# Masked attention on one core: the symmetric scores made once, their maxima sent through DRAM

## The chip, the cores and the metric

The kernel runs on one core of a Trainium2 chip. The metric is the device time of one execution, in microseconds. The core has four engines that compute: TensorE (PE in the profile; PEld is its loading of weights), VectorE (DVE), ScalarE (ACT) and GpSimd (POOL). SyncE (SP) issues the transfers between DRAM and the core's memory. Each engine works through its own list of instructions in order, and waits where an operand or a buffer isn't ready. TensorE writes its results into PSUM, eight banks of 512 float32 per partition.

## The reference

Four layers follow each other, all in float32. B is 8 samples, a sample is 256 x 512, and each layer's result goes on to the next with a residual. The change is in the first one, with 8 heads of 32 channels over 512 positions:

```python
q = xt @ Wq.T
scores = scale * jnp.einsum('bhqd,bhkd->bhqk', qh, qh)
cmask = mask[:, None, None, :]
rmask = mask[:, None, :, None]
logits = (scores * cmask + (1.0 - cmask) * NEG) * rmask
attn = jax.nn.softmax(logits, axis=-1)
ctx = jnp.einsum('bhqk,bhkd->bhqd', attn, qh)
out = ctx @ Wo.T
```

Queries and keys are the same vectors, so the scores of a head are a symmetric matrix. The mask takes keys away (cmask), and a masked query (rmask) weighs all keys alike: its context is the mean over the positions. The second layer is a modulated attention without a mask (16 heads, 256 positions), the third a scan of 256 time steps of an oscillator network, and the fourth a recurrent cell (GRU) over the same steps. The last two run as one loop, the scans.

## The kernel before

The program has two parts. The first, `attention`, does the first two layers for the eight samples; the second, `scans`, does the two scans. The second part starts when the first is done.

`attention` is one loop over steps g, from -5 to 78, with the instructions of each step written out in a fixed order (`manual_schedule`), so every engine's list follows the order of the calls. A sample takes U = 8 steps of masked attention: two halves e of four heads each, four steps per half. `at(g, rel, 8)` gives the sample b and the place in its eight steps for work that is rel steps late. The modulated attention of a sample runs about ten steps behind, so that in a step the two layers of neighbouring samples alternate on all engines.

The masked attention of sample b, by steps:

- `load` (g = 8b - 7): x and the mask row, the latter broadcast to all partitions (`mk`).
- `project` (8b - 5, 8b - 4): q for one half (`psq`), masked (`qm`, on VectorE) and copied (`qt`, on ScalarE); `project_out` turns it into `qtok` a step later.
- `maxima0` (from 8b - 4 on): scores of 128 positions against all 512, one PSUM bank per head (tile `n`, L204), and a maximum over each bank by VectorE (L209) into `mxp0`. After four steps `rows0` turns the maxima into rows (`pm`, `mrow`).
- `weights0` (from 8b on): the scores once more, transposed, with columns for 256 queries at a time (tile `s`, L226). A second product with two rows (L231) adds the mask and takes the maximum away inside PSUM. Its operands are `neg` and `mrow`. ScalarE's Exp (L238) writes `ex`.
- `values0` (8b + 1 to 8b + 9): the products of `ex` with the values and with ones (`pc`, L153), in two halves, and `weigh0` with a reciprocal and a product on VectorE.
- `masked_out` (8b + 9): the output projection (`pso`) and the residual.

The modulated attention follows: `normalize`, `modulate`, six `qkv` parts (`psqkv`), each of q and k normalized by `qkv_norm` (a reduction `s16` on VectorE, then three GpSimd instructions, one of them a pow, ending with `qr`) and turned by `qkv_out` in the next step (`ptqk`); then for each of four groups of heads `maxima1`, `rows1`, `weights1`, `values1`; and `modulated_out` (`psx`) with `modulated_turn` (`ptx`), which writes into `x2T`. That tile, 32 KB in each partition, holds the attention's whole result for the scans.

Seven PSUM banks go round for all of this (`bank`), and one is held for `pc` of the masked attention. At step 65 the tiles of the masked attention are given up and `follow` loads the scans' weights into their place.

Of the kernel before, what the change touches and what calls it, by code (L numbers as in the profile page):

```python
# [14 lines left out]
P = 128  # L15
# [9 lines left out]
def attention(ctx, tc, cst, x, cond, wqT, woT, w_emb, b_emb, g_norm, w_qkv, g_q, g_k, w_out, x2T, follow):  # L25
# [27 lines left out]
    ps_s = ctx.enter_context(tc.tile_pool(name="a_ps_s", bufs=7, space=PSUM))  # L53
    ps_c = ctx.enter_context(tc.tile_pool(name="a_ps_c", bufs=1, space=PSUM))

    def bank(shape, name):
        return ps_s.tile(shape, F32, tag="s", name=name)
# [3 lines left out]

    xs, mks = {}, {}

    def load(b):
        xs[b] = two.tile([P, 2, D], F32, tag="x", name=f"x_{b}", bufs=4)
        nc.sync.dma_start(xs[b], x[b].rearrange("(k p) t -> p k t", p=P))
        mks[b] = fone.tile([P, D], F32, tag="mk", name=f"mk_{b}")
        nc.sync.dma_start(mks[b], cond[b].partition_broadcast(P))
# [35 lines left out]

    rowm = wp.tile([P, 3], F32, name="rowm")
    nc.vector.memset(rowm, 0.0)
    nc.vector.memset(rowm[:, 1:2], 1.0)
    nc.vector.memset(rowm[:, 2:3], -1.0)
    for h in range(4):
        nc.vector.memset(rowm[32 * h : 32 * h + 1, 0:1], NEG)  # L110
        nc.vector.memset(rowm[32 * h : 32 * h + 1, 1:2], -NEG)
        nc.vector.memset(rowm[32 * h : 32 * h + 1, 2:3], 1.0)
# [48 lines left out]
    def weigh(pc, out, n):  # L161
        r = sm.tile([P, 256], F32, tag="r", name=f"r_{n}", bufs=2)
        nc.vector.reciprocal(r, pc[:, 1, :])
        nc.vector.tensor_mul(out, pc[:, 0, :], r)


    qms, qtoks, negs, mrows, exs0, ctxTs = {}, {}, {}, {}, {}, {}

    def project(b, e):
        if e == 0:  # L170
            qms[b] = ftwo.tile([P, 2, D], F32, tag="qm", name=f"qm_{b}")
            qtoks[b] = ftwo.tile([P, NJ, 256], F32, tag="qtok", name=f"qtok_{b}")
            negs[b] = ftwo.tile([P, D], F32, tag="neg", name=f"neg_{b}")
        ps = bank([P, D], f"psq_{b}_{e}")
        for k in range(2):
            nc.tensor.matmul(
                ps, lhsT=wq_sb[:, k, e * P : (e + 1) * P], rhs=xs[b][:, k, :], start=(k == 0), stop=(k == 1)
            )
        nc.vector.tensor_mul(qms[b][:, e, :], ps, mks[b])
        qt = line(f"qt_{b}_{e}")  # L180
        nc.scalar.copy(qt, ps)
        if e == 0:
            nc.gpsimd.tensor_scalar(negs[b], mks[b], rowm[:, 0:1], rowm[:, 1:2], ALU.mult, ALU.add)
        return qt
# [6 lines left out]

    def maxima0(b, e, qc):

        if qc == 0:
            nc.gpsimd.tensor_copy(
                mxp0[e].rearrange("p q (h i) -> p q h i", i=32)[:, :, :, 0],
                condT[:, :, b].unsqueeze(2).to_broadcast([P, NJ, 4]),
            )
        qm = qms[b]
        ss = []  # L200
        for h in range(4):
            r = 32 * h
            s = bank([P, D], f"n0_{b}_{e}_{qc}_{h}")
            nc.tensor.matmul(  # L204
                s, lhsT=qm[r : r + 32, e, qc * P : (qc + 1) * P], rhs=qm[r : r + 32, e, :], start=True, stop=True
            )
            ss.append(s)
        for h in range(4):
            nc.vector.tensor_reduce(mxp0[e][:, qc, 32 * h + 1 : 32 * h + 2], ss[h], AX.X, ALU.max)  # L209

    def rows0(b, e):
        pt = bank([P, NJ, P], f"pm0_{b}_{e}")
        for qc in range(NJ):
            nc.tensor.transpose(pt[:, qc, :], mxp0[e][:, qc, :], ident)
        mrows[b, e] = ftwo.tile([P, D], F32, tag="mrow", name=f"mrow0_{b}_{e}")
        nc.scalar.activation(mrows[b, e], pt.rearrange("p q n -> p (q n)"), AF.Copy, scale=rowm[:, 2:3])

    def weights0(b, e, qh, kp):
        qm, neg, mrow = qms[b], negs[b], mrows[b, e]
        qs = slice(256 * qh, 256 * qh + 256)  # L220
        ss = [bank([P, 2, 256], f"s0_{b}_{e}_{qh}_{kp}_{h}") for h in range(4)]
        for i in range(2):
            kc = slice((2 * kp + i) * P, (2 * kp + i + 1) * P)
            for h in range(4):
                r = 32 * h
                nc.tensor.matmul(  # L226
                    ss[h][:, i, :], lhsT=qm[r : r + 32, e, kc], rhs=qm[r : r + 32, e, qs], start=True, stop=False
                )
            for h in range(4):
                r = 32 * h  # L230
                nc.tensor.matmul(  # L231
                    ss[h][:, i, :], lhsT=neg[r : r + 2, kc], rhs=mrow[r : r + 2, qs], start=False, stop=True
                )
        exs = exs0.setdefault((b, e, qh), [])
        exs.append([])
        for h in range(4):
            ex = ftwo.tile([P, 2, 256], F32, tag="ex", name=f"ex0_{b}_{e}_{qh}_{kp}_{h}", bufs=12)
            nc.scalar.activation(ex, ss[h], AF.Exp, scale=SC)  # L238
            exs[-1].append(ex)

    pc0s = {}

    def values0(b, e, qh, half):
        if half == 0:
            if (e, qh) == (0, 0):
                ctxTs[b] = fone.tile([P, 2, D], F32, tag="ctxT", name=f"ctxT_{b}")
            pc0s[b, e, qh] = ps_c.tile([P, 2, 256], F32, tag="c", name=f"pc0_{b}_{e}_{qh}")
        pc = pc0s[b, e, qh]
        o = e * P
        values(pc, half, lambda k, h: qtoks[b][:, k, o + h * DH : o + (h + 1) * DH], exs0[b, e, qh])  # L250

    def weigh0(b, e, qh):
        pc = pc0s[b, e, qh]
        weigh(pc, ctxTs[b][:, e, qh * 256 : (qh + 1) * 256], f"0_{b}_{e}_{qh}")
# [159 lines left out]
    def modulated_turn(b, m, x2):  # L414
        pt = bank([P, NJ, P], f"ptx2_{b}_{m}")
        for j in range(NJ):
            nc.tensor.transpose(pt[:, j, :], x2[:, j * P : (j + 1) * P], ident)
        nc.scalar.copy(x2T[:, :, b, m * P : (m + 1) * P], pt)
# [6 lines left out]
    for b in range(B):  # L425
        per = 2 if b >= B - 2 else 1
        norms.append(U * b + U + (1 if b == B - 1 else 2))
        start = norms[b] + (2 if b != B - 2 else 3)
        for i, part in enumerate(PARTS):
            parts.setdefault(start + i // per, []).append((b, *part))  # L430
        HEADS.append(start + len(PARTS) // per)
        OUT.append(HEADS[b] + 6)
# [19 lines left out]
    with tc.manual_schedule():  # L452
        for g in range(-5, OUT[-1] + 3):
# [8 lines left out]
            if a := at(g, 0, U):  # L462
                weights0(a[0], a[1] // 4, a[1] // 2 % 2, a[1] % 2)
# [5 lines left out]
            if a := at(g, U + 1):  # L469
                masked_out(a[0])  # L470
# [9 lines left out]
            if a := heads(g, 1):  # L480
                rows1(*a)
            a, a1 = at(g, -4, U), heads(g, 0)
            soon = a and a[1] % 4 == 3
            if a and soon:
                maxima0(a[0], a[1] // 4, a[1] % 4)
            if a1 and not soon:
                maxima1(*a1)
            for part, lines in made:
                if lines:
                    qkv_norm(*part, *lines)  # L490
                    left["qkv", *part] = lines[1]
            if a2 := heads(g, 2):
                values1(*a2)
            if a2 := heads(g, 1):
                weights1(*a2)

            if (a2 := at(g, 1, U)) and a2[1] % 2 == 0:
                values0(a2[0], a2[1] // 4, a2[1] // 2 % 2, 0)
            behind = None
            if (a2 := at(g, 2, U)) and a2[1] % 2 == 0:  # L500
                behind = a2[0], a2[1] // 4, a2[1] // 2 % 2
                values0(*behind, 1)
            if a and not soon:
                maxima0(a[0], a[1] // 4, a[1] % 4)
            if a1 and soon:
                maxima1(*a1)
            if behind:
                weigh0(*behind)
            if soon:
                rows0(a[0], a[1] // 4)  # L510
            if (a2 := at(g, -7)) and a2[0] > 1:
                load(a2[0])
            if g == U * B + 1:
                first.close()
                follow()

# [390 lines left out]
def tile_kernel(  # L907
# [9 lines left out]
    x2T = cp.tile([P, NJ, B, T], F32, name="x2T")  # L917
# [34 lines left out]
    with ExitStack() as a:  # L952
        def follow():
            pool = ctx.enter_context(tc.tile_pool(name="s_weights", bufs=1, side="right", reuse_waits="tile"))
            cst["weights"] = scan_weights(pool, nc, cT, w_ih, w_hh)

        attention(a, tc, cst, x, cond, wqT, woT, w_emb, b_emb, g_norm, w_qkv, g_q, g_k, w_out, x2T, follow)
    with ExitStack() as s:
        scans(s, tc, cst, bias, b_ih, b_hh, x2T, out)
# [42 lines left out]
```

## Time and profile before

| | us |
|---|---|
| median of three runs | 3042.43 |
| lowest, highest | 3040.55, 3043.27 |
| profiled execution, its own time | 3040.15 |
| its span in the profile | 3038.4 |
| first instruction of the scans' loop (ic, L698) | 961.38 |
| last masked_out (first residual add, L264) | 853.92 |

Times inside the profile count from the start of the span. PE is busy 94% of the span, DVE 66%, ACT 53%, POOL 32%. The granted TensorE clock is 0.986 of full speed on the mean. The page divides the span into 40 slices of 76 us and gives each a digit, the busy share in tenths. A line of a group reads: line, engine, operation, what it writes and reads, count, then busy time in all and the mean ns of one, then the idle time of the engine just before it and what ended that. TensorE's float32 products stand as two records each in the trace.

### The profile page before, as it was taken

The page shows a single profiled execution, that of the slowest core. Times are in us where ns is not written, and L with a number is a line of the kernel's source. Part 1 is how long each engine was busy: PE and PEld are TensorE (multiplying, and loading weights), DVE is VectorE, ACT ScalarE, POOL GpSimd, SP SyncE. Part 2 cuts the span into 40 slices and gives each one's busy share as a digit, 9 for nine tenths or more (in the row PEclk, how much of TensorE's full clock was granted, in tenths as well). Part 3 has the DMA queues.
Part 4 walks back from the last instruction along what each step waited for, and adds up shares of the span by engine and source line. Part 5 has one row for each costly group of instructions (what it writes and reads, how often), then busy time and mean ns, then how long its engine had stood idle before and what let it go on. Part 6 is the DMA issues. An engine that isn't in the chain of part 4 may idle for free.

```text
span 3038.4 us, 165918 instructions
## 1 busy us (share of the span) xinstructions
PE 2847.2 (94%) x70330; PEld 2070.0 (68%) x70330; DVE 2002.5 (66%) x9090; ACT 1599.9 (53%) x8347; POOL 986.8 (32%) x2905
## 2 busy tenths in 40 slices
PE   8999999999988899999999999999999999999997
PEld 5455555555545677777777777777777777777775
DVE  4444444544434677777777777777777777777774
ACT  2333433433433566666666666666666666666652
POOL 0021111111221344444444444444444444444442
PEclk8999999999999999999999999999999999999999
DMA  3000000000040000000000000000000000000000
GB/s 129 5 1 1 12 11 1 12 11 1 2 98 2 4 7 6 7 6 6 7 6 7 6 6 7 6 7 6 6 7 6 7 6 6 7 6 7 6 6 7
DMA packets 17759, 35.31 MB, mean 12 GB/s; under 512 B 2144, under 2 KB 10860, under 8 KB 17012
## 3 DMA queue, kind: packets, MB, share of 16 engines
q1 hardware_dynamic: 17012, 24.69, 3.0%
q8 instruction: 550, 9.01, 1.2%
q14 instruction: 197, 1.61, 0.2%
HBM read 20.49 MB, written 4.19 MB: 8 GB/s over the span
## 4 chain that ended last, share of the span: by engine, by line
PE 62%; DVE 26%; ACT 6%; issue 4%; POOL 2%; ACTq 0%; DMA 0%; SPq 0%; POOLq 0%; DVEq 0%
PE pg L733 19%; PE ic L698 17%; PE psqkv L301 5%; DVE icT L890 5%; PE pc L153 5%; DVE qn L891 5%; ACT tT L598 4%; DVE hqs L851 3%; PE s L226 3%; DVE own L748 3%; DVE sqmm L847 2%; PE n L204 2%; DVE v L750 2%; PE psx L401 2%; DVE mxp L209 2%
## 5 line engine op out<-in xcount | busy, mean ns | idle before, releaser
L698 PE MATMUL ic<-cT_sb,tT 128*8 128x128 f32 x32736 | 1088.6, 273 | 82.2 <-ACT tT L598 44.6
L698 PEld LDWEIGHTS ic<-cT_sb,tT 128*8 128x8 f32 x32736 | 758.6, 89 | 344.0 <-ACT tT L598 272.0
L733 PE MATMUL pg<-whh_sb,hz 128*32 128x128 f32 x24576 | 818.5, 274 | 50.7 <-DVE hz L778 17.5
L598 ACT ACTIVATE tT<-qn 128x16 f32<-128x16 f32 x2046 | 440.2, 216 | 646.0 <-DVE qn L891 567.5
L733 PEld LDWEIGHTS pg<-whh_sb,hz 128*32 128x32 f32 x24576 | 667.4, 110 | 125.0 <-DVE hz L778 124.8
L890 DVE STREAM_TRANSPOSE icT<-ic 128x64 f32<-128x64 f32 x2048 | 503.7, 246 | 70.5 <-PE ic L698 64.9
L891 DVE SCALAR_TENSOR_TENSOR qn<-icT,hqs 128x16 f32<-128x16 f32 x2048 | 350.4, 171 | 70.1
L693 POOL TENSOR_TENSOR W<-W,cx 128x128 f32<-128x128 f32 x765 | 297.2, 389 | 256.7 <-ACT cx L679 256.7
L686 POOL TENSOR_TENSOR W<-cx,us 128x128 f32<-128x128 f32 x255 | 117.1, 459 | 446.1 <-ACT cx L679 446.1
L847 DVE SCALAR_TENSOR_TENSOR sqmm<-sqmm,qn 128x32 f32<-128x32 f32 x768 | 153.5, 200 | 152.2 <-ACT sqmm L836 123.1
L209 DVE TENSOR_REDUCE mxp<-n 128x1 f32<-128x512 f32 x256 | 158.7, 683 | 132.0 <-PE n L204 132.0
L851 DVE TENSOR_TENSOR hqs<-W,sqmm 128x32 f32<-128x32 f32 x1020 | 200.1, 196 | 46.1 <-DVE own L773 1.0
L238 ACT ACTIVATE ex<-s 128x512 f32<-128x512 f32 x256 | 132.1, 603 | 157.0 <-PE s L231 157.0
L712 PE MATMUL gi<-wih_sb,x3T 128*32 128x384 f32 (+2 forms) x3072 | 202.4, 379 | 0.5 <-POOL x3T L903 0.5
L324 POOL TENSOR_SCALAR r<-s 128x16 f32<-128x16 f32 x32 | 6.5, 204 | 604.0 <-DVE s L322 603.7
L679 ACT ACTIVATE cx<-qn 128x32 f32<-128x32 f32 x1280 | 200.9, 213 | 0.1
L301 PE MATMUL psqkv<-wqkv_sb,xnT 128*128 128x512 f32 x384 | 181.8, 620 | 0.0
L679 ACT ACTIVATE cx<-p 128x32 f32<-128x32 f32 x1020 | 149.8, 217 | 32.2 <-DVE p L846 1.4
L356 DVE TENSOR_REDUCE mxp<-n 128x2 f32<-128x512 f32 x128 | 79.6, 685 | 107.7 <-PE n L348 107.7
L226 PE MATMUL s<-qm 32*128 32x256 f32 x1024 | 139.4, 406 | 6.8 <-DVE mxp L209 6.8
L679 ACT ACTIVATE cx<-q 128x32 f32<-128x32 f32 x1020 | 145.5, 213 | 0.0
L748 DVE STREAM_TRANSPOSE own<-pg 128x128 f32<-128x128 f32 x256 | 84.9, 332 | 91.3 <-PE pg L733 91.3
(149 smaller groups left out, 3593.5 us busy)
## 6 DMA issues: line engine op xcount, KB each, us to landing
x<-in_x SPq DMA_DIRECT2D x8, 512.0 KB
out<-o SPq DMA_DIRECT2D x256, 16.0 KB
wqkv_sb<-in_L_cond_W_qkv SPq DMA_DIRECT2D x1, 3072.0 KB
wih_sb<-in_L_cond_W_ih SPq DMA_DIRECT2D x4, 768.0 KB
whh_sb<-in_L_cond_W_hh SPq DMA_DIRECT2D x4, 768.0 KB
mk<-in_cond SPq DMA_DIRECT2D x8, 256.0 KB
wemb<-in_L_cond_W_emb SPq DMA_DIRECT2D x4, 512.0 KB
wout_sb<-in_L_cond_W_out SPq DMA_DIRECT2D x1, 1024.0 KB
```

Of the source, the lines that this page charges most:

```text
L209: nc.vector.tensor_reduce(mxp0[e][:, qc, 32 * h + 1 : 32 * h + 2], ss[h], AX.X, ALU.max)
L226: nc.tensor.matmul(ss[h][:, i, :], lhsT=qm[r : r + 32, e, kc], rhs=qm[r : r + 32, e, qs], start=True, stop=False)
L301: nc.tensor.matmul(ps, lhsT=xnTs[b][:, c, m * P : (m + 1) * P], rhs=wqkv_sb[:, c, part * D : (part + 1) * D], start=(c == 0), stop=(c == N ...
L598: nc.scalar.activation(tT, src[:, half * HM : (half + 1) * HM, :], AF.Tanh)
L679: nc.scalar.activation(c[:, i], x, AF.Copy, scale=f)
L693: nc.gpsimd.tensor_tensor(W[:, i + 1 : 5], W[:, i + 1 : 5], c, ALU.add)
L698: nc.tensor.matmul(ps[32 * j : 32 * j + B, :], lhsT=tT[k // HM][:, k % HM, :], rhs=cT_sb[:, k, j * P : (j + 1) * P], start=(k == 0), stop= ...
L733: nc.tensor.matmul(pg_ps[rows(j), :], lhsT=hzs[tau % 3][:, k, 32 * g : 32 * g + 32], rhs=whh_sb[:, k, g, j * P : (j + 1) * P], start=((k, ...
L847: stt(mm, sq, LIN[s], qs, ALU.subtract, ALU.mult)
L851: nc.vector.tensor_sub(hq, W[:, s], mm)
L890: nc.vector.transpose(icT.rearrange("p m n -> p (m n)"), ic[:, half * 64 : half * 64 + 64])
L891: stt(qn[:, m2, :], icT[:, :, 0:B], IC[s], hq[:, m2, :], ALU.mult, ALU.add)
```

## The change

- `scores0` makes the scores of 128 positions against all 512 once (L198 of the changed kernel), and ScalarE copies the four heads' banks into a tile `sc` of 4 x 512 per partition (L203). Six such tiles are kept, so the scores stay from the step in which they are made until their products with the values.
- `maxima0` reduces all four heads in one VectorE instruction, from `sc` (L208).
- `rows0` turns the maxima as before, copies them, stores the four rows (8 KB) in DRAM and loads them back broadcast over the 128 partitions into `bc` (1 MB). Both transfers are SP's.
- `weights0` subtracts `bc` from `sc` on VectorE, in place (L226), and then takes one Exp over 4 x 512, with the key mask as a bias per partition (`negT`, L227). Because the scores are symmetric, the tile that was reduced along its rows serves here as its own transpose. It comes one step later than before.
- `values0` runs every step, with 512 queries at a time; two PSUM banks are held for it, and six go round.
- `weigh0` takes two reciprocals and two products on VectorE for a half, and three GpSimd instructions put the mean of q into the masked queries. The mean comes from the accumulator of `qt`'s copy. `rowm`, `neg`, and the rank-2 products are gone.
- Two buffers for `mk` instead of one.
- `x2T` moves into the memory that the masked attention gives up. Results that are ready before that go to DRAM (`x2d`, eleven stores of 256 KB) and are loaded back behind the scans' weights.
- The order of the calls in a step is changed: `values0` comes first, `qkv_norm` before `rows1` and `maxima1`; everything behind `weights0` is one step later.

```diff
-    ps_s = ctx.enter_context(tc.tile_pool(name="a_ps_s", bufs=7, space=PSUM))
+    ps_s = ctx.enter_context(tc.tile_pool(name="a_ps_s", bufs=6, space=PSUM))
...
-        mks[b] = fone.tile([P, D], F32, tag="mk", name=f"mk_{b}")
+        mks[b] = fone.tile([P, D], F32, tag="mk", name=f"mk_{b}", bufs=2)
...
-        qt = line(f"qt_{b}_{e}")
-        nc.scalar.copy(qt, ps)
-        if e == 0:
-            nc.gpsimd.tensor_scalar(negs[b], mks[b], rowm[:, 0:1], rowm[:, 1:2], ALU.mult, ALU.add)
+        qt = line(f"qt_{b}_{e}")
+        means[b, e] = sm.tile([P, 1], F32, tag="mean", name=f"mean_{b}_{e}")
+        nc.scalar.activation(qt, ps, AF.Identity, accum_out=means[b, e])
+        nc.gpsimd.tensor_scalar_mul(means[b, e], means[b, e], -1.0 / D)
...
+    def scores0(b, e, kc):
+        qm = qms[b]
+        ss = [bank([P, D], f"s0_{b}_{e}_{kc}_{h}") for h in range(4)]
+        for h in range(4):
+            r = 32 * h
+            nc.tensor.matmul(
+                ss[h], lhsT=qm[r : r + 32, e, kc * P : (kc + 1) * P], rhs=qm[r : r + 32, e, :], start=True, stop=True
+            )
+        sc = ftwo.tile([P, 4, D], F32, tag="sc", name=f"sc_{b}_{e}_{kc}", bufs=6)
+        for h in range(4):
+            nc.scalar.copy(sc[:, h, :], ss[h])
+        scs[b, e, kc] = sc
+
+    def maxima0(b, e, qc):
+        nc.vector.tensor_reduce(
+            mxp0[e].rearrange("p q (h i) -> p q h i", i=32)[:, qc, :, 0], scs[b, e, qc], AX.X, ALU.max
+        )
...
+        mrow = ftwo.tile([P, D], F32, tag="mrow", name=f"mrow0_{b}_{e}", bufs=1)
+        nc.scalar.copy(mrow, pt.rearrange("p q n -> p (q n)"))
+        bc = bcs[b, e] = ftwo.tile([P, 4, D], F32, tag="bc", name=f"bc_{b}_{e}")
+        row = dram.tile([4, D], F32, tag="row", name=f"row_{b}_{e}", bufs=2)
+        nc.sync.dma_start(row, mrow.rearrange("(h i) n -> h i n", i=32)[:, 0, :])
+        nc.sync.dma_start(bc, row.rearrange("h n -> (h n)").partition_broadcast(P).rearrange("p (h n) -> p h n", h=4))
+
+    def weights0(b, e, kc):
+        sc = scs[b, e, kc]
+        nc.vector.tensor_sub(sc, sc, bcs[b, e])
+        nc.scalar.activation(sc, sc, AF.Exp, bias=negT[:, kc, b : b + 1], scale=SC)
...
+    def weigh0(b, e):
+        fill = ftwo.tile([P, D], F32, tag="fill", name=f"fill_{b}_{e}", bufs=1)
+        nc.gpsimd.tensor_scalar(fill, mks[b], -1.0, means[b, e], ALU.add, ALU.mult)
+        cx = ctxTs[b][:, e, :]
+        pv, pn = pc0s[b, e]
         for i in range(2):
...
+            nc.vector.reciprocal(r, pn[:, t])
+            nc.vector.scalar_tensor_tensor(cx[:, t], r, 1e30, pv[:, t], ALU.min, ALU.mult)
+        nc.gpsimd.tensor_tensor(cx, cx, mks[b], ALU.mult)
+        nc.gpsimd.tensor_tensor(cx, cx, fill, ALU.add)
...
+        o = line(f"x2o_{b}_{m}")
+        nc.scalar.copy(o, pt.rearrange("p j n -> p (j n)"))
+        x2d[b, m] = dram.tile([P, D], F32, name=f"x2d_{b}_{m}")
+        nc.sync.dma_start(x2d[b, m], o)
...
-        norms.append(U * b + U + (1 if b == B - 1 else 2))
+        norms.append(U * b + U + (2 if b == B - 1 else 3))
...
-            if a := at(g, 0, U):
-                weights0(a[0], a[1] // 4, a[1] // 2 % 2, a[1] % 2)
+            if a := at(g, 2, U):
+                values0(a[0], a[1] // 4, a[1] % 4)
+            if a := at(g, -4, U):
+                scores0(a[0], a[1] // 4, a[1] % 4)
+            if a := at(g, 1, U):
+                weights0(a[0], a[1] // 4, a[1] % 4)
+            if (a := at(g, 2, U)) and a[1] % 4 == 3:
+                weigh0(a[0], a[1] // 4)
...
-            if g == U * B + 1:
+            if g == U * B + 2:
                 first.close()
                 follow()
+                for (b, m), d in x2d.items():
+                    nc.sync.dma_start(
+                        cst["x2T"][:, :, b, m * P : (m + 1) * P], d.rearrange("p (j n) -> p j n", j=NJ)
+                    )
```

## The prediction

> **What bounds the kernel now.** I read the page first, then busy time by stretches, then the chain of waits inside one stretch, then the groups with their shapes over the first 1150 us.
>
> ```profile
> PE   8999999999988899999999999999999999999997
> DVE  4444444544434677777777777777777777777774
> ACT  2333433433433566666666666666666666666652
> ...
> PE 62%; DVE 26%; ACT 6%; issue 4%; POOL 2%; ACTq 0%; DMA 0%; SPq 0%; POOLq 0%; DVEq 0%
> ```
>
> A slice is 76 us. In slices 2 to 11 TensorE is full while VectorE and ScalarE stand at four and three tenths; from slice 14 on it is another program. The timeline puts the border at 961.4 us, where the scans' first product (ic, L698) starts; the change touches only what is ahead of it. By stretches (columns: busy us and count for PE, PEld, DVE, ACT, POOL, then granted clock, DMA share, GB/s):
>
> ```profile
> 400.00:500.00 100.00, 98.47 (x922) 54.51 (x921) 48.06 (x67) 39.30 (x78) 14.42 (x14) 1.00 0.03 9
> 500.00:600.00 100.00, 97.66 (x912) 54.22 (x908) 46.48 (x66) 37.59 (x74) 14.82 (x16) 0.98 0.03 9
> ```
>
> TensorE is busy 98 of 100 us at full clock. The timeline gives the period of a sample: qm's first product (L179) starts at 327.17, 439.75, 552.36 and 664.99 us, so **112.6 us for 8 steps**. The chain of waits over 621 to 734 us is nearly all PE; one step of it:
>
> ```profile
> 626.08 3.43 PE psx L401 x8
> 629.51 1.86 PE pc L153 x32
> 631.37 1.07 PE n L204 x8
> 632.45 0.59 PE ptx L417 x4
> 633.03 1.25 PE s L226 x6
> 634.28 0.02 PE s L231 x3
> ...
> 635.37 0.43 PE s L231 x5
> 635.80 0.58 PE ptqk L336 x4
> 636.39 3.58 PE pso L261 x8
> ```
>
> Here n (the scores for the maxima) takes 1.07 us, and the second making of the scores with the rank-2 products (L226, L231) runs from 633.03 to 635.80: 2.77 us. In seven steps of this sample that I measured it is 2.4 to 2.9. The groups that the change replaces:
>
> ```profile
> L209 DVE TENSOR_REDUCE mxp<-n 128x1 f32<-128x512 f32 x256 | 158.7, 683 | 132.0 <-PE n L204 132.0
> L226 PE MATMUL s<-qm 32*128 32x256 f32 x1024 | 139.4, 406 | 6.8 <-DVE mxp L209 6.8
> L238 ACT ACTIVATE ex<-s 128x512 f32<-128x512 f32 x256 | 132.1, 603 | 157.0 <-PE s L231 157.0
> ```
>
> **What the Trainium skill says.** (1) "VectorE: DVE Perf Modes", section The perf-mode tier table: a float32 tensor_tensor and a reduction run in the 1x mode, one element per cycle, 2293 ns for the former at 2048 elements. The trace agrees at 512: 691 ns for a tensor_tensor (L179), 683 for the reduction. (2) "ScalarE: Activation LUTs", section What ACT_TABLE_LOAD costs: 280 ns plus 0.833 ns an element with a bias from memory; for 2048 that is an estimate of 1.99 us. The trace has 603 ns at 512 without such a bias. (3) "DMA: Bandwidth & Descriptors", section Anatomy of one DMA: about 2.0 us plus bytes over 436 GB/s. Here x and mk (0.77 MB, mk a broadcast of one row) are issued at 422.81 and 423.29 and the rings are empty again by about 426.6, at 393 GB/s in the fullest microsecond: agrees. (4) "SBUF — State Buffer", section Who interferes with whom: a VectorE instruction with two SBUF inputs and a GpSimd instruction that reads SBUF exclude each other for a whole instruction. No instruction of the attention part before is a large one of that kind, so the trace cannot show it.
>
> **The change, part by part.**
>
> *TensorE.* L226 and L231 go: 64 steps of 2.8 us, 179 us in all, 22.4 a sample. The scores of scores0 are what n was (1.07 a step). values0 streams the same columns (16 products of 512 instead of 32 of 256): 1.86 a step, nothing gained.
>
> *VectorE.* Out: four reductions, 2.48 us a step. In: one reduction of 4x512, the 683 ns of 512 plus 1536 elements at the page's one per cycle of 0.96 GHz, 2.28, and the subtraction, 2.29. Net +2.1 a step, +17 a sample: from 53.5 (47.5% of 112.6) to about 70 us.
>
> *ScalarE.* Out: four Exp, 2.06 a step. In: four copies, the same 2.06, and one Exp of 2048, 1.99. Net +16 a sample: from 44 to about 60. The accumulator of qt's copy adds some 0.06 (L273 against L314).
>
> *GpSimd.* Three 512-wide instructions per half sample (0.77 to 1.05 us by L183 and L326), 5 a sample; neg and the copy of condT go. Hidden behind the next step, since masked_out comes a step after weigh0.
>
> So TensorE stays the bound: 112.6 - 22.4 = 90 us. What it then waits for, per sample:
>
> - After psx the chain is: x2 add 0.69, s16 0.68 on DVE, then 0.2 + 2.9 + 1.05 on POOL, until ptqk may start: 6.3 us (404.2 to 410.5 in the timeline). Today pc, n, ptx and s cover it: 1.86 + 1.07 + 0.6 + 2.8. Without s, 2.7 us are open, in two steps: **+5.4**. In the step without psx about +1.
> - GpSimd's order puts weigh0's two last instructions (2 us) ahead of the pow of that step, and rows1's copy on ScalarE stands behind an Exp that waits for the subtraction, with six score banks in place of seven: +2 (0 to 5).
> - Moving qkv_norm ahead of rows1 and maxima1 takes away the wait of ptqk on POOL after four reductions (724.44 to 733.06 in the chain; PE idle 2.6): -2.6.
> - The exclusion of (4): the subtraction comes when the pow (2.9 us) runs, and qr's product (1.05) may then wait for the subtraction (2.29). Between 0 and 3 x 2.3; I take +3.
>
> 90 + 5.4 + 1 + 2 - 2.6 + 3 = **99 us a sample, 13.6 less**.
>
> *The added wait.* The subtraction waits for bc: copy 0.6, store of 8 KB 2.4 with its issue, load of 1 MB 0.4 + 4.4: 7.8 us. Behind it in VectorE's queue stand weigh0, qm, the maxima and norms; behind its Exp on ScalarE the evacuations of qkv. rows0 is two steps ahead, so one whole step (9 us or more in the steady part) and VectorE's backlog of 2 to 4 us cover it: 0 there. With thin steps it is open, see the start.
>
> *SP.* For samples 4 to 7 the load of x waits for the x2 add of a step later than now, one step before its projection: 3.8 us to land against 3.6 of TensorE plus the 2.7 above. 0 taken, up to +3 four times. The stores of x2o (eleven, 256 KB) stand between; nobody waits. The eleven reloads (2.9 MB) follow the scan's weights, which now move at 205 GB/s up to 882 us: 14 us more (28 at half the rate), covered by the 107 us between the last masked_out (853.9) and the scans.
>
> *The sum, against qm's starts now.* Up to sample 2's projection (128.0): bc is behind 7 MB of loads (DMA share 1.0 up to about 33 us), so the first subtraction comes near 40 and sample 1's projection 8 us late. Then steps have no qkv in them, and each is the loop Exp, values0, scores0, four copies, next Exp: 2.0 + 1.86 + 1.07 + 2.1, 7.1 us with starts, against 8 now (102.5 to 118.6 is two). I take -1 (-12 to +12). From 128.0 to 216.1: steps of 7 to 12 us as loop, weigh0 (4.3) and POOL allow, 72 in place of 88: -16 (-22 to -8). Four periods up to 665.0: -54 (-80 to -28). From 665.0 to 853.9: 13 steps lose their s, -22, and one more step's worth of Exp, weigh0 and GpSimd stands at the end, +8: -14 (-30 to 0). The rest up to 961.4: one bank fewer, +3 (0 to +8). The scans: no instruction changes, 0. Together **-82** (-144 to -16). The profiled execution took 3040.15 (span 3038.4 and 1.75 around it), the median of three is 2.3 above it: 3040.15 - 82 + 2 = **2960 us**.
>
> **Rivals.** (A) *TensorE keeps nearly all*: no exclusion, chains better covered than I drew: 179 less the 35 that the start and the end don't give, about 2900. For it: VectorE and ScalarE have 20 us a sample to spare. Against: the fixed 6.3 us chain. (B) *VectorE and GpSimd take over*: its 70 us become 80 by the lock, and in the step with weigh0 (subtraction 2.3, weigh0 4.3, reduction 2.3, maxima1 2.7, weigh 2.2: 13.8 against TensorE's 12.3, counted alike) it sets the pace; about 107 a sample, 5.6 less than now for some six samples, 3008. For: strict order and thin slack; against: the neighbouring steps have 2 to 4 us of room. (C) *Slower: the broadcast of bc is slow*, since 128 partitions read the same 8 KB of DRAM. Sixteen waits, each able to stop VectorE, then ScalarE, then TensorE. The cover is about 12 us; each 1 us beyond it costs 16. It decides from 17 us of bounce on (16 x 5 eats the 82); at 20 us the time is 3086. Against it: mk's broadcast of a 2 KB row moves with x at 393 GB/s. (D) *The change doesn't remove the second scores*: excluded, no product with mrow is left in the code.
>
> **How the numbers follow.** Forecast (2925 to 2990) 0.60; A 0.14; B 0.17, most of it short of 3036; C 0.07; between, within 0.2% (6 us, about what a measurement of this kernel can tell from no change), 0.02. Faster 0.91, same 0.02, slower 0.07. The range goes from a little below the low end of the sum (2898; in A the ramps may lose less than 35) to a little short of the high one (3026): 2885 to 3022.
>
> **What would show it.** Right: qm's starts about 99 us apart; the scans' first product near 880; no L226 or L231 group; 64 subtractions at 2.29 us, 64 reductions near 2.28 and 64 Exp near 1.99; new idle of TensorE ahead of ptqk, released by POOL. Wrong: subtractions above 3 us (the lock), VectorE idle on DMA bc in the steady part (C), TensorE idle on Exp or on copies of sc.

## The result, and the profile after

The changed kernel ("after") takes 3008.11 us, the median of four runs (3004.87 to 3012.63), beside 3041.54 for the kernel before on the same chip: ratio 0.9891, 95% interval 0.9873 to 0.9908. It is faster, by 33 us where 82 were forecast; 3008 lies inside the range, near its upper end. The profiled execution took 3006.1 us with a span of 3004.3, so 34.1 less span than before. The executions of one kernel lie 2 to 11 us apart, and each trace below is one of them, so a few us between two traces mean something only where the trace shows what made them.

The page of after, the same rows as before, then the shares of the chain that ended last:

```profile
PE   6679889888998999999999999999999999999997
DVE  4657667766535777777777777777777777777774
ACT  4456555655335666666666666666666666666652
...
PEclk7789999999999999999999999999999999999999
...
PE 55%; DVE 27%; ACT 8%; issue 4%; POOL 4%; ACTq 0%; DMA 0%; POOLq 0%; SPq 0%; DVEq 0%
```

The first three slices carry the surprise. TensorE, at 8, 9, 9 before, is at 6, 6, 7, and its granted clock, at 8, 9, 9 before, is at 7, 7, 8. From slice 4 on TensorE is at 8 and 9. The stretches show the same (columns: PE, PEld, DVE, ACT, POOL busy and count, granted clock, DMA share, GB/s). The first is in the start of after, the second is one whole steady period of after, the third one of before:

```profile
90.00:100.00 10.00, 5.92 (x28) 1.20 (x27) 7.11 (x4) 3.94 (x5) 4.90 (x3) 0.67 0.00 0
436.45:535.23 98.78, 87.02 (x652) 40.21 (x653) 69.01 (x59) 57.24 (x94) 25.38 (x22) 1.00 0.10 36
439.75:552.36 112.61, 109.93 (x1034) 61.03 (x1032) 53.23 (x74) 43.05 (x84) 18.57 (x17) 0.98 0.03 8
```

The groups of the first part (0 to 930 us) that replace those shown of before:

```profile
L226 DVE TENSOR_TENSOR sc<-sc,bc 128x2048 f32<-128x2048 f32 x64 | 150.1, 2345 | 4.3 <-DMA bc<-row 4.3
L208 DVE TENSOR_REDUCE mxp<-sc 128x4 f32<-128x2048 f32 x64 | 145.7, 2279 | 28.1 <-ACT sc L203 28.1
L203 ACT COPY sc<-s 128x512 f32<-128x512 f32 x256 | 131.1, 604 | 139.4 <-PE s L198 139.4
L227 ACT ACTIVATE sc<-sc,negT 128x2048 f32<-128x2048 f32 x64 | 129.5, 2024 | 22.6 <-DVE sc L226 15.1 <-issue 7.1
```

The four durations are within 3% of their prices (2.29, 2.28, 0.60 and 1.99 us). The wait for bc is 4.3 us in the whole run, once.

Where did the time go? The six stages of the prediction's sum, from the starts of qm's first half (samples 2, 3 and 7), the last masked_out and the scans' first ic, in us of the spans against before. E6 is an experiment of those below; it repairs both places where time was lost.

| stage | before takes | predicted | after | E6 |
|---|---|---|---|---|
| up to sample 2's projection | 128.0 | -1 | +14.9 | -9.5 |
| sample 2 to sample 3 | 88.1 | -16 | +6.3 | -11.4 |
| samples 3 to 7, four periods | 448.9 | -54 | -49.5 | -51.4 |
| sample 7 to the last masked_out | 188.9 | -14 | -5.4 | -10.6 |
| up to the scans | 107.5 | +3 | +1.4 | -5.4 |
| scans | 2077.0 | 0 | -1.9 | +1.6 |
| span | 3038.4 | -82 | -34.1 | -86.7 |

The scans are the same instructions in all the kernels, and take 2074.1 to 2079.0 us in the traces. The steady part came out nearly as predicted. Of the 48 us missed, 38 lie ahead of sample 3's projection. In the chain of waits of after, the start reads like this (start, duration, engine, tile, line):

```profile
87.81 1.90 ACT sc L227
...
89.82 3.64 PE pc L238 x16
93.46 1.88 PE s L198 x8
95.34 2.05 ACT sc L203 x4
97.39 1.90 ACT sc L227
...
99.33 3.64 PE pc L238 x16
102.98 2.02 PE s L198 x8
```

This is the loop that the prediction named: Exp, values0 (pc), scores0 (s), four copies, next Exp. But it goes round in 9.6 us, not 7.1. Exp and copies are as priced. values0 takes 3.64 in place of 1.86 and scores0 1.88 to 2.02 in place of 1.07: both run at about half speed. TensorE stands idle for 4 us in each round while ScalarE copies and takes the Exp.

From sample 2 to 3, where qkv comes in, the chain of after is another one:

```profile
196.16 0.50 ACT sq L318
...
196.69 0.70 DVE s L326
...
197.75 2.91 POOL r L329
...
200.72 1.96 POOL qr L330
...
202.72 1.11 PE ptqk L340 x4
203.84 5.35 PE psqkv L305 x8
```

One step of this chain is 13.05 us (sq at 196.16, the next at 209.21). TensorE comes to ptqk, the turn of qr, waits there for GpSimd, and only then makes the next psqkv, on which the next qr depends.

### The profile page after: what moved, and what is told of

Read it like the earlier page. It is cut to its first block, busy times and chain, and to the rows that moved or that the text cites. A ratio compares the mean times of both kernels' runs of the same rounds, so it can differ in the third digit from the quotient of the medians.

```text
span 3004.3 us, 159873 instructions
## 1 busy us (share of the span) xinstructions
PE 2713.9 (90%) x67258; PEld 1922.1 (64%) x67258; DVE 2129.0 (71%) x8948; ACT 1715.9 (57%) x8427; POOL 1047.1 (35%) x2945
## 4 chain that ended last, share of the span: by engine, by line
PE 55%; DVE 27%; ACT 8%; issue 4%; POOL 4%; ACTq 0%; DMA 0%; POOLq 0%; SPq 0%; DVEq 0%
PE pg L742 19%; PE ic L707 17%; DVE icT L899 5%; DVE qn L900 5%; PE psqkv L305 4%; ACT tT L607 4%; PE pc L238 3%; DVE hqs L860 3%; DVE own L757 3%; DVE sqmm L856 2%; DVE v L759 2%; POOL r L329 2%; PE s L198 2%; PE pc L154 2%; DVE hz L787 2%
## 5 line engine op out<-in xcount | busy, mean ns | idle before, releaser
L707 PE MATMUL ic<-cT_sb,tT 128*8 128x128 f32 x32736 | 1087.5, 273 | 82.4 <-ACT tT L607 44.3
L742 PE MATMUL pg<-whh_sb,hz 128*32 128x128 f32 x24576 | 818.9, 274 | 49.5 <-DVE hz L787 16.2
L203 ACT COPY sc<-s 128x512 f32<-128x512 f32 x256 | 131.1, 604 | 139.4 <-PE s L198 139.4
L208 DVE TENSOR_REDUCE mxp<-sc 128x4 f32<-128x2048 f32 x64 | 145.7, 2279 | 28.1 <-ACT sc L203 28.1
L226 DVE TENSOR_TENSOR sc<-sc,bc 128x2048 f32<-128x2048 f32 x64 | 150.1, 2345 | 4.3 <-DMA bc<-row 4.3
L227 ACT ACTIVATE sc<-sc,negT 128x2048 f32<-128x2048 f32 x64 | 129.5, 2024 | 22.6 <-DVE sc L226 15.1
L845 ACT ACTIVATE sqmm<-qn 128x32 f32<-128x32 f32 x768 | 140.5, 183 | 0.6
```

Of the source, the lines that this page charges most:

```text
L707: nc.tensor.matmul(ps[32 * j : 32 * j + B, :], lhsT=tT[k // HM][:, k % HM, :], rhs=cT_sb[:, k, j * P : (j + 1) * P], start=(k == 0), stop= ...
L742: nc.tensor.matmul(pg_ps[rows(j), :], lhsT=hzs[tau % 3][:, k, 32 * g : 32 * g + 32], rhs=whh_sb[:, k, g, j * P : (j + 1) * P], start=((k, ...
```

## The experiments

All ratios are against the kernel before on the same chip (its medians were 3041 to 3044 us). The theory was that the start's loop, and ptqk's place ahead of work that doesn't need it, took the 38 us. The rivals were that the subtraction took them (VectorE's load, and its lock on GpSimd: the exclusion of point (4) of the prediction), the clock alone, the transfers of the start, or that a gain in the start is given back later whatever is done.

**E1, scores0 ahead of values0 in every step.**

```diff
+            scores0 ...     # called ahead of values0
             values0 ...
-            scores0 ...
-        sc = ftwo.tile(..., bufs=6)
+        sc = ftwo.tile(..., bufs=7)
-        mrow = ftwo.tile(..., tag="mrow", bufs=1)
+        mrow = line(f"mrow0_{b}_{e}")
```

> scores0 is called ahead of values0 in each step, with seven sc tiles in place of six (mrow takes a line tile, to make room). Loop theory: in the thin steps of samples 0 and 1 (up to qm of sample 3, 237.3 us in the changed kernel) each step is the chain Exp, values0, scores0, copies, next Exp, 9.6 us long; with the scores first the copies no longer wait for the Exp of the step before, a step falls to what VectorE needs (2.3 + 2.3 + a quarter of 4.3 = 5.7) or to TensorE's 5.7 at the low clock, and the thin part gets 25 to 50 us shorter; the steady period stays within 2 us of 98.8. Total 2955 to 2985. Bounce theory (the waits for bc set the thin steps): under 8 us gained, about 3000. Lock theory (subtraction against GpSimd): nothing in the thin part, about 3006.

Measured: 3008.73 us, ratio 0.988 [0.9866, 0.9895]; no gain over after. The stages tell why: sample 3's projection is at 211.2 in place of 237.3, 26 us earlier, but the four periods take 421.5 us in place of 399.4 and the stretch up to the scans 113.8 in place of 108.9. The start was repaired and the steady part got longer with the same edit. TensorE doesn't wait more there, as one of E1's periods shows beside that of after above:

```profile
419.76:523.70 103.94, 92.93 (x652) 42.61 (x653) 68.67 (x59) 57.61 (x94) 25.41 (x22) 0.98 0.10 34
```

It waits 11.0 us in place of 11.8, and is busy 92.9 us with the 652 records that took 87.0. In all four periods it is busy 376.8 us in place of 353.0 and waits 44.7 in place of 46.4, and the granted clock is 0.94 to 0.98 in place of 0.97 to 1.00. Why the clock falls more often in this order stays open.

**E2, the clock.** Three unused products (128x128 by 512) behind scores0 in steps 1 to 12; nothing else.

```diff
+            if 1 <= g <= 12:
+                keep(g)     # three matmuls into a bank that nobody reads
```

> Steps 1 to 12 of the changed kernel get three more products of 128x128 by 512 behind scores0, whose result nobody reads (0.86 us each at full clock, 2.6 a step). Loop theory with the clock in it: values0 takes 3.64 and scores0 2.0 in these steps because the granted clock is 0.5 to 0.67; with TensorE kept busy they take 1.86 and 1.07, a step falls from 9.6 to about 7.1, and sample 2's qm comes at about 120 in place of 142.9: total 2980 to 2990. If the low clock is not what sets the steps, the products cost 0 to 2.6 us a step and nothing is gained: 3006 to 3030.

Measured: 3008.1 us, ratio 0.9877 [0.9859, 0.9894]. The chain of waits of E2 over the same microseconds:

```profile
90.96 1.92 PE pc L243 x16
92.88 1.15 PE s L198 x8
94.03 2.05 ACT sc L203 x4
96.08 1.90 ACT sc L232
...
98.03 1.92 PE pc L243 x16
99.95 1.15 PE s L198 x8
```

A round is 7.07 us: the price in the prediction is right at full clock, and the clock is the whole of a round's difference. Yet sample 2 comes only 6.3 us earlier, because the products themselves stand in the chain at 66.34, 122.91 and 132.04 us, 2.77 us each; without these 8.3 us the stage from sample 1 to 2 would take 70.2 in place of 78.5. Of the 6 us, 4.4 are left at the last masked_out; the stretch up to the scans takes 112.7 us in place of 108.9, with the same waits of TensorE (11.1 us) at a clock of 0.94 in place of 0.97.

**E3, qkv_out later.** The call of qkv_out goes from behind weigh0 (on TensorE: behind scores0) to behind modulated_out, so that projections, pso, qkv and psx come ahead of ptqk on TensorE.

```diff
-            for a in leave("qkv"):
-                qkv_out(*a)
...
                     left["x2", b, g - OUT[b]] = modulated_out(b, g - OUT[b])
+            for a in leave("qkv"):
+                qkv_out(*a)
```

> qkv_out of the step before is called behind modulated_out, so TensorE no longer waits for GpSimd's pow and qr ahead of masked_out, project and qkv. If that wait costs what I put on it (5.4 + 1 a sample, and more in samples 0 and 1, where the chain qkv, sq, s16, pow, qr, ptqk is all there is in a step: about 3 us in each of four steps), the steady period falls from 98.8 to 92 to 94, the thin part by about 8: total 2960 to 2975. If TensorE's wait there only moves to another place (banks, VectorE), the period stays at 97 to 99: 2995 to 3006.

Measured: 2979.42 us, ratio 0.9789 [0.9774, 0.9803], 29 us less than after. Sample 2 to 3 takes 82.4 us in place of 94.4; sample 3 to the last masked_out 575.8 in place of 583.0; up to the scans 102.1 in place of 108.9. Neither expectation holds as a whole: the total is near the first one's, the period near the second's (397.7 for four, 99.4 each). In the period the wait mostly changed its place (9.6 us on the mean in place of 11.6, and 1.6 us more of TensorE's work at a lower clock), as the groups of PE over 420 to 520 us show (last column: idle before, releaser), against ptqk in after:

```profile
L352 PE MATMUL n<-kT,qT 32*128 32x256 f32 x64 | 5.4, 442 | 4.7 <-ACT qT L344 4.7
```

```profile
L340 PE MATMUL ptqk<-ident,qr 128*128 128x128 f32 x16 | 2.6, 286 | 6.1 <-POOL qr L330 6.1
```

The first line is E3's, the second that of after over one period (436.45 to 535.23).

**E4, no subtraction.** The maximum isn't taken away; this leaves 64 VectorE instructions of 2.3 us out of the computation.

```diff
-        nc.vector.tensor_sub(sc, sc, bcs[b, e])
```

> The subtraction is left out: Exp takes the scores as they are, all else stays (maxima, DRAM, bc). Lock theory and VectorE theory: 2.3 us a step leave VectorE and no qr product waits for its port (it took up to 1.95 us in place of 1.05); if these set the steady period it falls by 5 to 15 us a sample, total 2920 to 2970. Loop theory: the steady period falls by 2 to 4 only (the qr products), the thin steps stay at 9.6 since Exp still waits for the copies behind it; the first step no longer waits for bc (33.6 to 40.7), 5 us: total 2980 to 2998.

Measured: 2984.35 us, ratio 0.9805 [0.979, 0.9819]. VectorE's load falls from 69.0 to 51.0 us a period, but the period only from 99.9 to 98.2: **VectorE isn't the bound**. The start's rounds stay at 9.6 us (one took 8.4) and at clock 0.66, so the subtraction isn't their cause either. The total lies where the loop theory had it. The subtraction still costs 24 us in all by the medians. In the trace without it 5.8 us are gained up to sample 1's projection, where nothing waits for bc now, 8.3 from sample 2 to 3, and 14.1 from there to the last masked_out; 3.8 are lost again up to the scans, with the same waits of TensorE at a clock of 0.94 in place of 0.97. The lock shows in GpSimd's product qr, one line of after and one of E4 (duration min/median/max in ns):

```profile
L330 POOL TENSOR_TENSOR qr<-qr,r x32: 1046/1052/1947, 187.8 to 877.4; 128x512 f32<-128x512 f32 x32
```

```profile
L329 POOL TENSOR_TENSOR qr<-qr,r x32: 1046/1047/1050, 181.5 to 850.3; 128x512 f32<-128x512 f32 x32
```

With the subtraction some of these products take up to 0.9 us longer; without it none does. What happens shows where they meet (after, 199 to 204 us):

```profile
199.48 2.28 DVE L226 TENSOR_TENSOR sc<-sc,bc 128x2048 f32<-128x2048 f32 x1
200.72 1.95 POOL L330 TENSOR_TENSOR qr<-qr,r 128x512 f32<-128x512 f32 x1
```

The subtraction ends at 201.76, the product 0.91 us later, most of its own 1.05. So it is in all 15 cases of after in which the product starts while a subtraction runs: it ends 0.90 to 0.92 us behind it.

**E5, the order part alone.** The kernel before, with qkv_norm ahead of rows1 and maxima1.

```diff
+            for part, lines in made:      # ahead of rows1
+                if lines:
+                    qkv_norm(*part, *lines)
+                    left["qkv", *part] = lines[1]
             if a := heads(g, 1):
                 rows1(*a)
```

> The kernel before, with qkv_norm alone moved ahead of rows1 and maxima1 (the order part of the change, without kept scores). The step of the prediction: -2.6 us a sample in the steady part, so about 110 us between qm's first halves in place of 112.6, and 6 samples times 2.6 = 16 less in all: about 3026 us. Rival: VectorE's reductions for the maxima now come later and the wait moves to rows1's transposes: period 112 to 113, time within 0.2% of before.

Measured: 3030.42 us, ratio 0.9961 [0.9949, 0.9974]. That is 11 us, where 16 were expected. The steady periods hold only 5.9 of it, 1.5 each, of which 1.0 is TensorE's wait (1.7 us a period in place of 2.7); most of the rest lies between samples 2 and 3 (4.8) and after sample 7 (2.5).

**E9, the order undone in after.** qkv_norm back behind rows1 and maxima1.

> After, with qkv_norm moved back behind rows1 and maxima1, as in the kernel before (the one part of the order undone). By the prediction's step (-2.6 us a sample for the move, and -11 us for the same move in the kernel before): +11 to +21, about 3020 to 3028 us, with TensorE waiting more ahead of ptqk. Rival (VectorE is fuller in the changed kernel and the four reductions of maxima1 now stand between sq and s16 in every such step): more than +25. Other rival: the move is worth nothing here, within 5 us of after.

Measured: 3010.92 us, ratio 0.9897 [0.9876, 0.9918], the same as after. TensorE's wait at ptqk is 6.0 us over 436 to 535 us, against 6.1. The last of the three expectations holds: in the changed kernel the move is worth nothing that can be measured.

**E6, start and turn together.** After, with scores0 ahead of values0 in steps up to 12 only, and qkv_out late as in E3.

```diff
+            if g <= 12 and (a := at(g, -4, U)):
+                scores0(a[0], a[1] // 4, a[1] % 4)
             if a := at(g, 2, U):
                 values0(a[0], a[1] // 4, a[1] % 4)
-            if a := at(g, -4, U):
+            if g > 12 and (a := at(g, -4, U)):
                 scores0(a[0], a[1] // 4, a[1] % 4)
...              # seven sc tiles and mrow in a line tile as in E1; qkv_out as in E3
```

> After, with scores0 ahead of values0 in steps up to 12 only (a seventh sc tile), and qkv_out called behind modulated_out everywhere. Theory (the thin start is a loop of Exp, values0, scores0, copies, and the gains of the two edits add): sample 2's projection at 119 to 121 us, sample 3's at 201 to 205, the steady period as with qkv_out late alone (99 to 100), total 2955 to 2965 us. Rival (whatever the start gains is lost in the steady part, since samples start nearer to each other, as scores0 first everywhere did): about 2975 to 2982, as with qkv_out late alone.

Measured: **2957.41 us**, ratio 0.9726 [0.9705, 0.9747], the lower end of what the theory gave. Sample 2 is at 118.5, sample 3 at 195.2, 6 us earlier than the theory had it. In the page TensorE's first slices are fuller and the clock is higher:

```profile
PE   7689988998998999999999999999999999999996
...
PEclk8899999998999999999999999999999999999999
```

The loop is gone from the chain of waits in the start; what ends last there now is VectorE with 4.4 us per 128 positions, and then the bounce of the maxima through DRAM:

```profile
82.41 2.68 DVE sc L226
85.09 2.20 DVE mxp L208
87.29 2.20 DVE sc L226
89.48 2.21 DVE mxp L208
...
92.86 1.68 DMA row<-mrow
...
94.60 5.24 DMA bc<-row
```

**E11, the start alone.** E6 with qkv_out where after has it.

> After, with scores0 ahead of values0 in steps up to 12 alone (a seventh sc tile); qkv_out stays where after has it. Theory (the start's loop is the mis-sized term, and its gain stays if the order of the steady part is untouched): sample 2's projection at 118 to 121 us, sample 3's at 208 to 213, steady period 99 to 101 as in after, total 24 to 28 us less than after: about 2980 to 2985. Rival (an earlier start is given back in the steady part whatever its order, as when scores0 was first everywhere): 3003 to 3010.

Measured: 2989.4 us, ratio 0.9824 [0.9806, 0.9842], 19 us less than after: short of the 24 to 28 expected. Sample 2 is at 123.1 (expected 118 to 121), sample 3 at 216.8 (208 to 213), 20.5 us earlier than in after. Those 20.5 us are still there at the last masked_out (799.8 against 820.3) and at the scans' first ic (908.7 against 929.2), where E1 kept 5.5 and 0.6 of its 26. The four periods took 404.2 us in place of 399.4, but the stage behind them 178.8 in place of 183.6. What makes one period longer than another shows in two of E11's own:

```profile
317.14:415.86 98.72, 87.02 (x652) 40.21 (x653) 69.02 (x59) 57.25 (x94) 25.38 (x22) 1.00 0.10 36
517.28:620.95 103.67, 92.45 (x652) 42.48 (x652) 69.04 (x58) 57.30 (x94) 25.37 (x22) 0.95 0.10 34
```

The work is the same, TensorE waits 11.7 and 11.2 us, and it is busy 5.4 us longer at the lower clock. That is also most of why E11's sample 2 comes late: E1, E6 and E8 have the same order up to there, and have it at 118.5 to 119.2; from sample 1 on TensorE waits as long in all four (17.1 to 17.7 us), but the clock is 0.76 in E11 and 0.80 in the others. By the medians E3 gives 29 us, E11 19, both together (E6) 51. From sample 2 to 3, E6 takes 76.8 us where E3 takes 82.4, again with the same waits (15.8 and 15.7 us), at a clock of 0.93 in place of 0.85.

**E7, the start's transfers.** E6, with the loads of w_qkv and w_out (4 MB) issued in step -1, behind the first row and bc.

> The kernel with thin start and late qkv_out (scores0 ahead of values0 in steps up to 12, qkv_out behind modulated_out), and the loads of w_qkv and w_out issued in step -1, behind the first row and bc. Theory (the first subtraction waits for the row behind 4 MB of loads): row lands in about 1.7 us in place of 5.4, the first subtraction at 33 to 34 us in place of 38.3, sample 1's projection 4 to 5 us earlier, total 4 to 5 us less than without that edit. Rival: modulation's addition to w_out, or the first qkv, now waits for the loads, or the start is bound elsewhere: difference within 2 us, or slower.

Measured: 2956.89 us, ratio 0.9717 [0.9702, 0.9732], the same as E6: the rival. The first subtraction starts at 34.7 us (37.2 in E6) and sample 1's projection comes at 48.5 (49.9), but sample 2's is at 120.2 against 118.5: between them TensorE waits as long as in E6 (17.4 us), at a clock of 0.76 in place of 0.80. The row lands in 1.75 us; in this trace of E6, where it was issued 2.6 us later, behind the same loads as in after, it took 1.76.

**E8, the residual add earlier.** E6, with modulated_out ahead of weights0.

> The kernel with thin start and late qkv_out, and modulated_out (psx and its residual add x2) called ahead of weights0, so ahead of the subtraction and weigh0 in VectorE's queue and ahead of qkv on TensorE. Theory (in the two steps with psx VectorE runs behind: the x2 add started 4.6 us after psx would allow the turn, TensorE waited 1.4 to 4 us a sample there): period 97 to 98 in place of 98.7 to 99.1, last masked_out and total some 8 to 12 us earlier, about 2947. Rival (psx now stands ahead of qkv, so qkv's copies, norm and turn come 3.6 us later and the wait moves to ptqk or n): same within 3 us, or slower.

Measured: 2961.81 us, ratio 0.9736 [0.9718, 0.9753]: no gain. The periods are 100 to 101 us. The wait of ptx is gone, and in its place values0 waits for weigh0, which now stands behind the add on VectorE (groups of PE, 395 to 494 us):

```profile
L238 PE MATMUL pc<-sc,qtok 128*32 128x512 f32 x64 | 9.2, 652 | 3.0 <-DVE ctxT L256 3.0
```

**E10, clock and loop.** E6 with E2's unused products.

> The kernel with thin start and late qkv_out, and three unused products of 128x128 by 512 behind scores0 in steps 1 to 12, to keep TensorE's granted clock up. Theory A (in the shorter start the clock still costs: values0 and scores0 take 3.3 and 2.0 us in half of the steps, and the chain now runs through VectorE and the bounce of bc as well): sample 3's projection 3 to 8 us earlier than 195.2, total 2950 to 2955. Theory B (the start is now held by VectorE, bc and modulation, not by TensorE's duration): sample 3's projection within 3 us, total the same as without the products or a few us more.

Measured: 2965.67 us, ratio 0.9747 [0.9731, 0.9762], some 8 us slower than E6. This is nearer to theory B, but sample 3 comes 11.9 us later, not within 3. Sample 2 comes 9.9 us later. With the loop broken, the clock costs less than the products do.

## Why the prediction was right in sign and wrong in size

Two terms of the sum failed, "-1" for the start and "-16" for the stage behind it; together they hold 38 of the 48 us missed.

- **The second scores (right).** TensorE's busy time fell from 109.9 us in one period before (439.75 to 552.36) to 87.0, 22.9 less; 22.4 were predicted. (The two periods had a clock of 0.98 and 1.00; before's period from 216 to 327, at 1.00, has 108.4, so 21.4 of it are work.) No product with mrow is left, so rival D is out.
- **The steady period (right, by terms that partly cancel).** 99 us predicted, 99.9 on the mean of four. TensorE's waits add up to 11.8: 6.1 at ptqk for GpSimd (6.4 predicted), 1.8 for the x2 add, 1.4 for maxima, 1.3 for qt, 1.2 for xh. None of them is for a bank; the "+2" for GpSimd's order and the banks wasn't measured by itself. The "-2.6" for qkv_norm's move is not there: E9 measured nothing in the changed kernel, E5 1.5 a period in the one before. I took it from one wait of 2.6 us behind sample 7's projection (724.44 to 733.06) and carried it to every sample; in a steady period of before (439.75 to 552.36) TensorE waits only 1.0 us at ptqk for GpSimd. Against that, "+3" for the lock was too much: in each of the four periods one product qr was held for 0.9 us, and without the subtraction TensorE waits 1.9 us a period less, lock and load taken together.
- **The start (wrong).** The prediction has "each is the loop Exp, values0, scores0, four copies, next Exp: 2.0 + 1.86 + 1.07 + 2.1, 7.1 us with starts, against 8 now" and from it "-1 (-12 to +12)". The loop was right and its size was not: 9.6 us. I took 1.86 and 1.07 from the full-clock steady part.

  What these two durations missed is the clock. The Trainium skill, "TensorE: Matmul & The Clock Gate", section Why this matters for your kernels, says that a gap of some 3 us between bursts drops TensorE to half rate. The trace agrees: the loop has gaps of 4 us, and values0 in it takes 3.64/1.86 = 1.96 times as long. The clock was down before the loop began: from 70 to 80 us, in modulation's small products (pe, 64 records, no gap), it is 0.55. In before it falls there too (0.69 from 60 to 70) and is back at 0.96 from 80 to 90; after's loop stays at 0.67 from 80 to 130, and with its gaps filled (E2) the clock is back at 1.00 from 90 on.

  From sample 1 to 2 six rounds run at half speed: 6 x 2.5 = 15, and that stage is 83.4 us where the prediction's own numbers give 127.0 - 58.4 = 68.6. E2 shows the clock as the cause of a round's length; E1, E6 and E11 show that the loop itself needn't be there.

  The 8 us for bc behind the first loads were right in size partly by luck: sample 1 came 9.1 us later, but E4, where nothing waits for bc, takes back only 5.8 of them, and E1 and E6, whose first subtraction still waits for bc until 38.1 and 37.2 us (38.3 in after), have sample 1 at 50.8 and 49.9, as before (50.4). The loop took its part here too.
- **"From 128.0 to 216.1 ... 72 in place of 88: -16" (wrong, and the larger miss: 22 us).** It took 94.4. I bounded these steps by the loop, weigh0 and GpSimd one by one. What ended last was their sum through ptqk: square, sum, pow, product, turn and the next psqkv in a row, 13 us, with psqkv at 5.35 in place of 3.6 at the reduced clock and qr at 1.96 in place of 1.05 under the lock. E3 takes 12.0 us out of this stage by the place of one call, E6 17.7.
- **The end, "-14".** It gave 5.4 in this trace, but the border at sample 7's projection moves with the clock: E9 and E11 take 404.1 and 178.9, 404.2 and 178.8 us for the four periods and this stage, where after takes 399.4 and 183.6, each time 583.0 together. For both together -68 was predicted and -54.9 measured. ptqk waits 9.7 us for GpSimd between 637 and 820 us (9.7 in E9 and E11 too), against 3.6 us between 665 and 854 before. The cover that s had given is gone here too, a term that I had put in the steady part only.
- **The tail and the scans (right).** +3 predicted and +1.4 measured; the scans' own 1.9 us less lie within what they differ by from trace to trace.
- **The rivals.** A is out: the waits are there. B gave 3008 us, what was measured, and is still false: VectorE is busy 69.0 of 98.8 us, the period is 99.9 and not 107, and E4's 18 us less VectorE work shorten it by 1.7. C is out: bc takes 3 to 5.5 us to land, and VectorE waited for it once. The formula of point (3) is given on that page for transfers that GpSimd issues; SP issues these, and the 8 KB store lands in 1.7 us where the formula gives 2.0.
- **A small reading.** The accumulator of qt's copy costs more than "some 0.06": behind each copy the trace has a record of 0.19 to 0.23 us that reads it.
- **What was given back.** After's time is set by a start 21 us later than before at sample 3, and four periods that win 49. The version with both repairs, E6, meets the predicted sum stage by stage to within 9 us (column above); its 2957 us being near the forecast of 2960 says nothing for the forecast, since it is another kernel.

Still open: what makes the granted clock fall for single stretches of the steady part. It makes periods of the same kernel 98.7 and 103.7 us long (E11), and in E1 it took back the whole gain of the start.

## What to carry to other kernels

Price the stage with few instructions in flight apart from the steady one, and take its durations at the clock that it will have: work removed from TensorE leaves gaps, and with gaps of 4 us values0 and scores0 took nearly twice as long. In a strict order, ask of each call which of the calls behind it needs it: moving one turn (E3) and one making of scores (E6), with no less work, gained 51 us, more than the 33 of the whole change. When two versions differ by a few us, set TensorE's waits apart from its busy time and the clock: here a period grew by 5 us with no more waiting. A step's cover is a property of its stage, so a wait found in one stage must not be multiplied by the number of samples.

## What the runs showed of the hardware

- In a steady rhythm of 5.5 us of work and 4 us of gap TensorE stayed at about half speed, for the 50 us from 80 to 130; with three unused products of 512 columns in the gap, 2.77 us, it was back at full speed from 90 on (values0 1.92 in place of 3.64 us, E2).
- In the steady part the granted clock falls now and then with waits that are no longer than elsewhere: the same 652 records took 87.0 us at 1.00 and 92.5 at 0.95 (E11).
- The Trainium skill, "SBUF — State Buffer", section Who interferes with whom, was named in the prediction with no trace to test it. The trace of after agrees: GpSimd's product of 512, started while a subtraction of 2048 ran, ended 0.90 to 0.92 us behind it in 15 of 15 cases, so it took up to 1.95 us in place of 1.05; without subtractions (E4) it never took more than 1.05.
- A store of 8 KB to DRAM took 1.7 us to land, but 5.37 when it was issued at 28.18 us behind the kernel's first loads, which kept the DMA engines full until 31 to 32. Issued behind the same loads at 29.29 us (E1) it took 3.87, at 30.69 (E6) 1.76: it landed at 32.5 to 33.6 each time.
